# Scores turned out of PSUM by VectorE, and four kinds of work one to two places later, in a graph-attention kernel on one core

## The chip, the core and the metric

The kernel runs on one core of one Trainium2 chip. A core has five engines with in-order instruction streams: TensorE (PE in the profile, PEld for its weight loads), VectorE (DVE), ScalarE (ACT), GpSimd (POOL), and SyncE (SP), which here only starts transfers. On-chip memory is SBUF and, for the results of matmuls, PSUM in banks of 128 partitions by 512 fp32 values. The metric is the device time of one execution in microseconds; the time of a kernel is the median of several runs.

## The reference

A layer norm and a relu feed one graph-attention layer over 12,500 nodes with 128 features and 412,500 edges with 64 features, sorted by `dst`. One softmax runs over all edges.

```python
h = jnp.maximum(_layernorm(x, axis=-1), 0.0)
# inside, with node_features = h:
h = node_features @ Wn + bn
q = node_features @ Wq + bq
k = node_features @ Wk + bk
v = node_features @ Wv + bv
eh = edge_features @ We + be
attn_in = jnp.concatenate([q[src], k[tgt], eh], axis=-1)
hmid = jax.nn.leaky_relu(attn_in @ A1 + b1, 0.2)
scores = jax.nn.leaky_relu(hmid @ A2 + b2, 0.2)            # 8 heads
w = jax.nn.softmax(scores.mean(axis=-1), axis=0)           # over all edges
out = jax.ops.segment_sum(w[:, None] * v[tgt], src, num_segments=num_nodes)
y = h + out
return x + gamma * (y - mean(y)) / jnp.sqrt(var(y) + 1e-5) + beta
```

## The kernel before

**Nodes and edges.** Nodes are cut into 98 blocks of 128. Edges come in 403 groups of 1024 (`SUPER` = 8 tiles of 128 edges), and the groups are cut into 11 chunks (`CHUNKS`). Within a chunk each edge is sent to a slot of its source's block, so that the second half of the work can go block by block.

**Three jobs, interleaved.** While chunk c is in the first stage, the second stage handles chunk c-1 and the slot planning (`ready`) works out chunk c+1. Python writes the program in the order in which these jobs give up their turns: `interleave` takes one step at a time from the job that is least far along. Between 1010 and 5300 us all three run together.

- *First stage* (`first_stage`): a step makes half a group's row, two tiles of 128 edges. TensorE multiplies edge features (L993) and adds selected key and value rows (L996) in one PSUM bank; ScalarE evicts the bank to a ring of rows (`evict`: L977 writes the edges' places, L980 the bank), and POOL scatters the two tiles to the slot table in DRAM (L910). `Later` holds the eviction back for a number of first-stage steps. Three banks take turns: two of `row_ps` and `t_bank` (`next_bank`).
- *Slot planning* (`count`, `plan`, `place_slots`): one-hot products on TensorE (L476, L497, L553, L575), with VectorE building the operands (L469, L568) and reducing the result (L631).
- *Second stage* (`second_stage`): works through units of up to four blocks, nearly all of 12 slot tiles in three quads of four tiles. A unit's rows are loaded into `rows_of`, a ring of 72 tiles (SP, L1024).

**A unit's steps.** `second_stage` keeps a table: `at(when, turn, job)` puts a job at a place, and within a place the lower turn is written first, then the earlier unit. With `t` as twice the unit's start, a unit goes through: `places` and `put_places` (source places transposed on TensorE at L1040 through a bank of `next_bank`, copied out by ScalarE at L1045, sent round through DRAM); `select` (one-hot selection `sel_q`, VectorE, L1064); for each quad, two places apart, `turn` (TensorE transposes the rows, L1074, and adds the query rows, L1079, in one of two `h_ps` banks) and `steep` (leaky relu: ScalarE makes 0.2 times the value in the single buffer `low`, L1088; VectorE takes the larger of both, L1089, into `rows_of`). Then `heads_of` (TensorE, L1096: scores of 8 heads, and in a ninth column their weighted sum, into the single bank `s_ps`), `add_bias` (ScalarE, L1103: bank plus b2 to `z` in SBUF), `by_slot` (VectorE transposes 32x32 blocks, L1109, so that edges lie on partitions) and `scores` (VectorE, L1116 to L1124). `spread_top` and `greatest` (L1129, L1138) find the running maximum through `s_ps`, `exponentials` (ScalarE, L1151 and L1155) the weights of the edges. With `lag` places after the start, `weights` (VectorE, L1169: one-hot of the place times the weight, `w`), `products` (TensorE, L1182: values summed by node into `o_ps`) and `add_sums` (VectorE, L1198, or L1190 in the first chunk) follow quad by quad.

A place that ScalarE, VectorE or TensorE is given in this table is its place in that engine's own stream; the engines meet through semaphores alone. The table in the lines that the change touches (before):

```python
at(t + 2 * q, 1, turn, i, q)
at(t + 2 * q + 1, 0, steep, i, q)
t += 2 * nq                      # nq: quads of a unit
at(t - 1, 3, heads_of, i)
at(t, 0, add_bias, i)
at(t + 1, -1, by_slot, i)
at(t + 1, -1, scores, i)
at(t + 2, 2, spread_top, i)
at(t + 2, 3, greatest, i)
at(t + 3, 2, exponentials, i)
t = 2 * w["start"] + w["lag"]
at(t + 2 * q - 1, 0, weights, i, q)
at(t + 2 * q, 1, products, i, q)
```

## Time and profile before

| what | value |
|---|---|
| median of 3 runs | 5679.47 us (5656.46 to 5683.55) |
| the profiled execution | 5691.83 us, span 5690.1 us |
| mean granted TensorE clock | 0.878 |
| busy, share of the span | PE 78%, DVE 70%, POOL 57%, PEld 55%, ACT 37% |
| moved by DMA | 1316.86 MB, 231 GB/s |
| first chunk alone with the nodes | until about 930 us |
| both stages and slot planning | about 1010 to 5300 us |
| last chunk's second stage, output | from about 5430 us |

A group of instructions in the profile is shown as: line, engine, operation, tile written <- tiles read, shape and count; behind the bar its busy time and the mean length of one in ns; behind the second bar the time that the engine sat idle just before these instructions and what ended most of it ("<-DVE w L1169 171.3": 171.3 us ended when VectorE's w of line 1169 was there; "issue": nothing that the profile shows; "remote": an event of no known engine). An fp32 matmul is two matmul rows in the profile, and names are printed without their numbers (`a2_sb` as a_sb, `b2_col` as b_col).

### The profile page before, as it was taken

To read this page: it belongs to the slowest core of one execution; us is meant where nothing else is said; L and a number is where in the kernel's file an instruction comes from. 1 tells how busy PE (TensorE), PEld (TensorE's weight loads), DVE (VectorE), ACT (ScalarE), POOL (GpSimd) and SP (SyncE) were. 2 spreads that over 40 slices of the span, in tenths; PEclk is the share of its full clock that TensorE was granted. 3 is DMA by queue.
4 is the path that set the end of the run, shared out by engine and by line. 5 is a ranking of instruction groups with operands and counts; after the bars stand their busy time and mean duration, and the time that the engine had idled before them with its cause. 6 is when DMAs were issued, how large, how long until landed. Compare 5 with 4: busy or idle time off the path is not lost. (4 is left out here: it accounts for less than half of the span.)

```text
span 5690.1 us, 88351 instructions
## 1 busy us (share of the span) xinstructions
PE 4417.7 (78%) x27227; PEld 3125.2 (55%) x27227; DVE 3969.6 (70%) x12757; ACT 2087.2 (37%) x5599; POOL 3235.7 (57%) x3250
## 2 busy tenths in 40 slices
PE   6766656787788787788878778778778777778898
PEld 4433334555555555555555556556556555556674
DVE  6777534777677766666776776776777676667898
ACT  2333322333333333333333333333333333334456
POOL 3556566666566666665656655665665665665510
PEclk8888867998889888888888988988888988889999
DMA  4657667777777777776777777776776776778985
GB/s 127 187 189 212 207 191 243 237 248 227 229 240 246 224 251 232 238 234 220 244 229 240 242 230 235 239 241 219 244 243 225 250 235 211 245 242 278 300 280 205
DMA packets 659520, 1316.86 MB, mean 231 GB/s; under 512 B 112886, under 2 KB 310443, under 8 KB 659023
## 3 DMA queue, kind: packets, MB, share of 16 engines
q1 hardware_dynamic: 453248, 848.70, 49.2%
q0 software_dynamic: 154704, 424.26, 19.9%
q10 hardware_dynamic: 51071, 38.02, 2.1%
q8 instruction: 220, 3.60, 0.3%
q14 instruction: 277, 2.27, 0.1%
HBM read 820.50 MB, written 490.10 MB: 230 GB/s over the span
## 5 line engine op out<-in xcount | busy, mean ns | idle before, releaser
L910 POOL DMA_INDIRECT tab<-row,slots x3223 | 3232.6, 1003 | 2206.2 <-ACT row L980 940.6
L1182 PE MATMUL o_ps<-rows_of,w 128*128 128x128 f32 x6860 | 1024.6, 294 | 320.9 <-DVE w L1169 184.0
L1182 PEld LDWEIGHTS o_ps<-rows_of,w 128*128 128x128 f32 x6860 | 917.9, 203 | 446.4 <-issue 204.1
L1169 DVE TENSOR_SCALAR w<-iota_f,rows_of,score 128x128 f32<-128x128 f32 x3381 | 954.8, 356 | 0.2 <-issue 0.2
L1089 DVE TENSOR_TENSOR rows_of<-h_ps,low 128x512 f32<-128x512 f32 (+1 forms) x861 | 589.3, 684 | 510.0 <-ACT low L1088 324.1
L980 ACT ACTIVATE row<-row_ps 128x512 f32<-128x512 f32 x1151 | 681.1, 594 | 681.6 <-remote 212.1
L1088 ACT ACTIVATE low<-h_ps 128x512 f32<-128x512 f32 (+1 forms) x861 | 512.2, 595 | 1099.4 <-remote 352.1
L993 PE MATMUL row_ps<-w_ea,ea_t 128*128 128x256 f32 x2302 | 811.6, 437 | 102.8 <-ACT row L980 69.3
L1079 PE MATMUL h_ps<-sel_q,qw 128*128 128x128 bf16 (+3 forms) x4242 | 769.8, 315 | 11.5 <-issue 11.3
L993 PEld LDWEIGHTS row_ps<-w_ea,ea_t 128*128 128x128 f32 x2302 | 429.5, 214 | 344.4 <-issue 182.5
L1096 PE MATMUL s_ps<-rows_of,a_sb 128*32 128x384 f32 (+2 forms) x2392 | 316.6, 608 | 353.8 <-DVE rows_of L1089 231.7
L1074 PE MATMUL h_ps<-ident,rows_of 128*128 128x128 f32 x3430 | 583.7, 296 | 8.5 <-issue 7.9
L996 PEld LDWEIGHTS <-sel 126*128 126x128 bf16 x3224 | 343.6, 107 | 296.8 <-issue 78.1
L1074 PEld LDWEIGHTS h_ps<-ident,rows_of 128*128 128x128 f32 x3430 | 456.3, 154 | 86.4 <-issue 45.8
L1079 PEld LDWEIGHTS <-qw 128*128 128x128 bf16 x4242 | 413.6, 104 | 142.3 <-issue 51.0
L996 PE MATMUL row_ps<-kv,sel 126*128 126x256 bf16 x2302 | 486.7, 295 | 5.7 <-issue 4.7
L1103 ACT ACTIVATE z<-s_ps,b_col 128x384 f32<-128x384 f32 (+1 forms) x299 | 169.6, 567 | 787.6 <-PE s_ps L1096 426.3
L631 DVE TENSOR_REDUCE num<-run 128x5 f32<-128x490 f32 (+1 forms) x648 | 425.5, 657 | 10.3 <-PE run L575 4.5
L970 DVE TENSOR_SCALAR sel<-offs,third 126x512 bf16<-126x512 uint8 x806 | 361.1, 489 | 68.2 <-remote 35.7
L575 PE MATMUL run<-one,rest_b 128*128 128x500 f16 x637 | 262.6, 412 | 177.2 <-DVE num L631 108.1
L1138 DVE TENSOR_SCALAR_CACHE_REDUCE s_ps<-s_ps,less_of 128x128 f32<-128x128 f32 x298 | 106.1, 356 | 410.3 <-PE o_ps L1182 110.0
L1064 DVE TENSOR_SCALAR sel_q<-pls,part 128x512 bf16<-128x512 uint8 (+1 forms) x837 | 366.4, 490 | 0.7 <-issue 0.7
(247 smaller groups left out, 4816.4 us busy)
## 6 DMA issues: line engine op xcount, KB each, us to landing
rows_of<-tab SPq DMA_DIRECT2D x264, 1542.0 KB
ea_t<-in_ea SPq DMA_DIRECT2D x403, 256.0 KB
qw<-q_tab SPq DMA_DIRECT2D x192, 384.0 KB
tab<-row,slots POOLq DMA_INDIRECT x3223
offs<-off_d SPq DMA_DIRECT2D x403, 126.0 KB
pls<-pl_d SPq DMA_DIRECT2D x264, 192.0 KB
rows_of<-tab SPq DMA_DIRECT2D x27, 1028.0 KB
qw<-q_tab SPq DMA_DIRECT2D x96, 288.0 KB
```

What stands on the lines that cost most here:

```text
L631: nc.vector.tensor_reduce(num, strips[:, :NTN, :m].rearrange("p b m -> p m b"), AX.X, ALU.max)
L910: i = nc.gpsimd.indirect_dma_start(out=tab[:, :], out_offset=bass.IndirectOffsetOnAxis(ap=slots[c][t // (8 * STR)][:m, t % (8 * STR):t % ( ...
L980: nc.scalar.activation(row[:, :, 1:ROW], bank, AF.Copy)
L993: nc.tensor.matmul(bank[:, :, 0:D], lhsT=ea_g[:, ts(k, P)], rhs=w_ea, start=True, stop=False, skip_group_check=True)
L996: nc.tensor.matmul(bank[:, b, :], lhsT=sel[:, ts(b * halves + k, P)], rhs=kv, start=False, stop=True, skip_group_check=True)
L1064: nc.vector.tensor_scalar(sel[:, a:b], plss[i][:, a:b], part1, None, op0=ALU.is_equal)
L1074: nc.tensor.matmul(h_ps[:, ts(j, P)], lhsT=rows_of[i][:, a + j, 1:D + 1], rhs=ident, is_transpose=True, start=j == 0, stop=False, skip_gro ...
L1079: nc.tensor.matmul(h_ps[:, (x0 - a) * P:(x1 - a) * P], lhsT=qws[i][:, s, ts(k, D)], rhs=plss[i][:, x0 * P:x1 * P], start=False, stop=k == ...
L1088: nc.scalar.activation(low, h_ps, AF.Copy, scale=SLOPE)
L1089: nc.vector.tensor_max(rows_of[i][:, a:b, 1:D + 1], h_ps.rearrange("p (j e) -> p j e", j=m), low.rearrange("p (j e) -> p j e", j=m))
L1169: nc.vector.tensor_scalar(w, iota_f, rows_of[i][:, t, 0:1], state["score", i][:, t:t + 1], op0=ALU.is_equal, op1=ALU.mult)
L1182: nc.tensor.matmul(state["o_ps"][:, ts(t // ct, D)], lhsT=w, rhs=rows_of[i][:, t, D + 1:ROW], start=t == 0, stop=t % ct == ct - 1, skip_gr ...
```

## The change

VectorE's transpose reads the scores from `s_ps` itself; ScalarE's step with b2 and the tile `z` are gone. b2 (with the weighted sum as ninth value) lies in all partitions as `b2_all`, and VectorE adds it to nine of every 32 columns behind the transpose. In the table, `steep` moves from one to two places behind its `turn`; `heads_of` moves two places later, `by_slot` and `scores` one, `spread_top`, `greatest` and `exponentials` two; `lag`, and with it `weights`, `products` and `add_sums`, becomes 2nq+7 in all chunks, where it was 2nq+5 in all but the last. Rows of units with more than two quads are loaded two places later. In the first stage the eviction is written two steps behind its matmuls instead of one, except in the first chunk.

```diff
-        lag = 2 * nq + (7 if c == NC - 1 else 5)
+        lag = 2 * nq + 7
...
-    b2_col = const.tile([P, 1], FP, name="b2_col")
+    b2_all = const.tile([P, H + 1], FP, name="b2_all")
...
-        nc.tensor.matmul(t_bank[:, 0:1], lhsT=b2_row.rearrange("p g h -> p (g h)"), rhs=ones[0:1, 0:1], start=True, stop=True)
-        nc.vector.tensor_copy(b2_col, t_bank[:, 0:1])
+        nc.tensor.matmul(t_bank[:, 0:H + 1], lhsT=ones[0:1, :], rhs=b2_row[:, 0:H + 1], start=True, stop=True)
+        nc.vector.tensor_copy(b2_all, t_bank[:, 0:H + 1])
...
-                later.after(1, lambda g=g, k=k, bank=bank: evict(g, k, bank))
+                later.after(1 if chunk_of[g] == 0 else 2, lambda g=g, k=k, bank=bank: evict(g, k, bank))
...
-        def add_bias(i):
-            n = 32 * units[i]["n"]
-            state["z"] = p3.tile([P, most_tiles * 32], FP, name="z")
-            nc.scalar.activation(state["z"][:, 0:n], state["s_ps"][:, 0:n], AF.Identity, bias=b2_col)
-
         def by_slot(i):
-            nc.vector.transpose(state["zt"][:, 0:n], state["z"][:, 0:n])
+            nc.vector.transpose(state["zt"][:, 0:n], state["s_ps"][:, 0:n])
...
-            zt = state["zt"][:, 0:32 * n].rearrange("p (t h) -> p t h", h=32)
+            zt = state["zt"][:, 0:32 * n].rearrange("p (t h) -> p t h", h=32)[:, :, 0:H + 1]
+            nc.vector.tensor_add(zt, zt, b2_all.unsqueeze(1).to_broadcast([P, n, H + 1]))
...
-                at(t + 2 * q + 1, 0, steep, i, q)
-            t += 2 * nq
+                at(t + 2 * q + 2, 0, steep, i, q)
+            t += 2 * nq + 2
...
-        t = 2 * w["start"] - (19 if w["nq"] > 2 else 17)
+        t = 2 * w["start"] - 17
```

The order of instructions shows what this does. The places are the same unit of the program before and after, where a chunk with quads of four tiles passes into one with quads of three. On TensorE before, from the last turn of a unit (`h_ps_36061`) to its heads (`s_ps`):

```order
L1079 MATMUL h_ps_36061<-sel_q_35872,qw_7833 128x384
L993 MATMUL row_ps_36076<-w_ea_200,ea_t_35643 128x2x128
...
L1182 MATMUL o_ps_36083<-rows_of_7832,w_36059 128x128
L1096 MATMUL s_ps_7834<-rows_of_7832,a2_sb_193 32x384 x4
L1074 MATMUL h_ps_36116<-ident_74,rows_of_7832 128x128 x3
```

and after, from the last turn of that unit (`h_ps_35852`):

```order
L1078 MATMUL h_ps_35852<-sel_q_35666,qw_7827 128x384
...
L1177 MATMUL o_ps_35727<-rows_of_7826,w_35847 128x128
...
L1073 MATMUL h_ps_35927<-ident_74,rows_of_7826 128x128 x3
...
L1177 MATMUL o_ps_35942<-rows_of_7826,w_35920 128x128
L1095 MATMUL s_ps_7828<-rows_of_7826,a2_sb_193 32x384 x4
L1039 MATMUL row_ps_35952<-ident_74,rows_of_7826 12x128
```

A whole turn of the next unit and another group of products now stand between a unit's last turn and its heads, and the heads stand in one place with `places` (L1039). On VectorE before, from the last w ahead of that unit's last max (L1089, out of `h_ps_36061`) on:

```order
L1169 TENSOR_SCALAR w_36059<-iota_f_154,rows_of_7832,score_35948 128x128
L1089 TENSOR_TENSOR rows_of_7832<-h_ps_36061,low_36080 128x4x128
L1064 TENSOR_SCALAR sel_q_36093<-pls_35911,part1_168 128x512
...
L1169 TENSOR_SCALAR w_36110<-iota_f_154,rows_of_7832,score_35948 128x128
L556 TENSOR_TENSOR run_36144<-run_36144,carry0_144 128x490
...
L1109 STREAM_TRANSPOSE zt_36161<-z_36112 128x384
L1116 TENSOR_TENSOR none_36163<-slot_of4_114,filled0_140 128x12
```

and after:

```order
L1164 TENSOR_SCALAR w_35920<-iota_f_154,rows_of_7826,score_35781 128x128
L1088 TENSOR_TENSOR rows_of_7826<-h_ps_35852,low_35922 128x4x128
L504 TENSOR_TENSOR filled3_143<-run_35902,carry0_144 128x98
...
L1164 TENSOR_SCALAR w_35968<-iota_f_154,rows_of_7826,score_35781 128x128
L1103 STREAM_TRANSPOSE zt_35970<-s_ps_7828 128x384
L1110 TENSOR_TENSOR none_35972<-slot_of4_114,filled0_140 128x12
L1114 TENSOR_TENSOR zt_35970<-zt_35970,b2_all_196 128x12x9
```

The max still follows a w and the transpose still follows the next ones; what moved is TensorE's side, and the transpose now reads TensorE's bank. On ScalarE before, around the copy of the places (L1045):

```order
L1103 ACTIVATE z_36112<-s_ps_7834,b2_col_196 128x384
L980 ACTIVATE row_255<-row_ps_36076 128x2x256
L1088 ACTIVATE low_36171<-h_ps_36116 128x384
L977 ACTIVATE row_255<-place1_233 128x4
L980 ACTIVATE row_255<-row_ps_36127 128x2x256
L1045 ACTIVATE plT0_36202<-t_bank_213 12x128
L1048 DMA pl_d_67<-plT0_36202 12x128
L980 ACTIVATE row_255<-row_ps_36183 128x2x256
```

and after (TensorE's order there is `t_bank`, the turn `h_ps_35927`, `row_ps_35938`, `places` in `row_ps_35952`, the turn `h_ps_35987`):

```order
L1087 ACTIVATE low_35981<-h_ps_35927 128x384
L1044 ACTIVATE plT0_35984<-row_ps_35952 12x128
L1047 DMA pl_d_67<-plT0_35984 12x128
L976 ACTIVATE row_252<-place1_230 128x4
L979 ACTIVATE row_252<-t_bank_213 128x2x256
L979 ACTIVATE row_252<-row_ps_35938 128x2x256
L1087 ACTIVATE low_36057<-h_ps_35987 128x384
```

z is gone, and the evictions of `t_bank` and `row_ps_35938` stand behind the copy of the places, whose matmul TensorE issues after theirs.

14 lines of the change are left out of this document (6 added, 8 removed).

## The prediction

> **What bounds the kernel now.** I read the page's shares, then the busy time by stretch, then for the longest stretch the instructions grouped by line for TensorE (PE), VectorE (DVE) and ScalarE (ACT), and last the order in time of one stall. By stretch (length, then busy microseconds of PE, weight loads, DVE, ACT, POOL; granted clock, DMA share, GB/s):
>
> ```profile
> 1010.00:5300.00 4290.00, 3415.36 (x21841) 2479.59 (x21842) 3017.07 (x9638) 1529.16 (x3928) 2596.01 (x2584) 0.89 0.73 238
> 5300.00:5430.00 130.00, 116.59 (x911) 92.48 (x910) 107.57 (x340) 55.99 (x150) 71.69 (x72) 0.97 0.89 295
> 5430.00:5620.00 190.00, 168.23 (x1442) 135.44 (x1441) 172.30 (x597) 112.15 (x318) 6.37 (x7) 0.98 0.77 250
> ```
>
> Three quarters of the time is the first row, in which both stages and the slot planning run together. There PE is busiest (3415 of 4290 us) and yet idle for 875 us (20.4%); DVE is at 70%, ACT at 36%, POOL at 61%, the DMA engines at 73%. No engine is full: they wait for each other. The second row, where the slot planning is over, shows PE idle for only 10.3%, at a clock of 0.97 instead of 0.89, so neither DMA (0.89 there) nor DVE (83% there) holds PE at its present pace.
>
> PE's groups in the long stretch (after the bar: busy time, mean ns; idle time just before them and what ended it):
>
> ```profile
> L1182 PE MATMUL o_ps<-rows_of,w 128*128 128x128 f32 x5925 | 891.6, 295 | 300.0 <-DVE w L1169 171.3 <-issue 74.9 <-DVE acc L1198 25.6
> L993 PE MATMUL row_ps<-w_ea,ea_t 128*128 128x256 f32 x1726 | 592.7, 427 | 37.8 <-ACT row L980 30.6 <-issue 5.3 <-ACT plT L1045 1.5
> L1074 PE MATMUL h_ps<-ident,rows_of 128*128 128x128 f32 x2964 | 509.0, 298 | 7.8 <-issue 7.2 <-PE t_bank L996 0.3
> L993 PE MATMUL t_bank<-w_ea,ea_t 128*128 128x256 f32 x856 | 296.5, 431 | 18.1 <-ACT row L980 11.5 <-issue 6.0 <-ACT plT L1045 0.6
> L1096 PE MATMUL s_ps<-rows_of,a_sb 128*32 128x384 f32 (+2 forms) x2008 | 279.6, 636 | 328.2 <-DVE rows_of L1089 207.6 <-issue 113.5 <-DVE num L631 4.6
> L575 PE MATMUL run<-one,rest_b 128*128 128x500 f16 x463 | 186.5, 403 | 120.2 <-DVE num L631 72.8 <-issue 39.7 <-DVE s_ps L1138 5.4
> ```
>
> The largest wait is at the heads (L1096), 328 us in 251 units (2008 matmuls, 8 to a unit): 1.31 us each, for the leaky values that DVE writes at L1089. Next the products (L1182), 300 us for w. What DVE and ACT wait for:
>
> ```profile
> L1089 DVE TENSOR_TENSOR rows_of<-h_ps,low 128x512 f32<-128x512 f32 (+1 forms) x744 | 509.0, 684 | 466.2 <-ACT low L1088 289.2 <-issue 170.1 <-ACT row L980 2.5
> L1198 DVE SCALAR_TENSOR_TENSOR acc<-acc,fade_of,o_ps 128x512 f32<-128x512 f32 (+3 forms) x246 | 156.7, 645 | 161.9 <-remote 58.4 <-PE row_ps L996 36.9 <-PE run L575 22.4
> L1109 DVE STREAM_TRANSPOSE zt<-z 128x384 f32<-128x384 f32 (+2 forms) x251 | 141.3, 563 | 103.0 <-ACT z L1103 87.2 <-issue 15.6
> L1138 DVE TENSOR_SCALAR_CACHE_REDUCE s_ps<-s_ps,less_of 128x128 f32<-128x128 f32 x252 | 89.9, 357 | 396.4 <-PE o_ps L1182 108.0 <-remote 64.4 <-PE h_ps L1079 59.5
> L1103 ACT ACTIVATE z<-s_ps,b_col 128x384 f32<-128x384 f32 (+2 forms) x251 | 144.6, 576 | 731.5 <-PE s_ps L1096 379.0 <-PE o_ps L1182 78.6 <-PE h_ps L1079 49.8
> ```
>
> So it is a ring: PE turns a quad, DVE waits for ACT's part of it (466 us at L1089), PE then waits for DVE at the heads, ACT waits for the heads at z with evictions queued behind it. One such stall in order of time (start, duration, engine and line, idle before):
>
> ```profile
> 3153.88 1.30 PE L1182 MATMUL o_ps<-rows_of,w 128*128 128x128 f32 x8 [1.31 <-DVE w L1169]
> ...
> 3155.39 0.95 DVE L970 TENSOR_SCALAR sel<-offs,third 126x512 bf16<-126x512 uint8 x2
> ...
> 3156.26 0.68 DVE L1089 TENSOR_TENSOR rows_of<-h_ps,low 128x512 f32<-128x512 f32 x1
> ...
> 3156.99 1.51 PE L1096 MATMUL s_ps<-rows_of,a_sb 128*32 128x384 f32 x8 [1.81 <-DVE rows_of L1089]
> ```
>
> Here DVE is the late one: it turns out sel before the leaky values, and PE has nothing it may do.
>
> **The change, part by part.** All times are in the long stretch unless said; the sum is made against the profiled execution, 5691.83 us (span 5690.1), 12 us above the median of 5679.47.
>
> *Leaky values and heads later.* A quad's max comes two places behind its turn instead of one, and the heads one place behind the last max instead of in its own place. That takes away the direct hop of L1096. What remains is what a one-place gap leaves now: w at L1169 stands one place ahead of the products, and these wait 300.0 us in 741 groups (5925/8), 0.40 each. For 251 heads that is 100 us. Bounds: 328 saved if nothing waits; nothing saved if PE is held by DVE's total work. I take the one-place price, as heads now follow the products directly and DVE's max follows that quad's w: **-228**.
>
> *DVE's own waits.* With two places between turn and max, most of the 466 us at L1089 should go: DVE gains up to 1.9 us a unit, PE 0.9. DVE so gets ahead of PE relative to today, which shortens the wait for w. Against it stands that PE now reaches the products sooner. Bounds: 300 saved, or 228 added (the heads' whole gain coming back). I take a fifth of the 300: **-60**.
>
> *z leaves ACT.* 144.6 us of ACT work and 731.5 us of its waiting vanish; ACT at 36% bounds nothing, so this is worth nothing by itself. But DVE now waits for the heads with its own queue (scores, max, w behind it), one place behind them. The nearest row is L1198, which waits for PE's products one place back: 161.9 us, against 103.0 that L1109 waits now. The 59 us more fall on DVE's idle time, which this stretch has in plenty (1273 us): nothing on the path, its cover being that PE has a turn and a row group to do meanwhile; 59 without it.
>
> *Transposing out of PSUM and the added b2.* Rows of the same size by form:
>
> ```profile
> L1109 DVE STREAM_TRANSPOSE zt<-z 128x384 f32<-128x384 f32 x264 | 150.3, 569 | 104.2 <-ACT z L1103 87.6 <-issue 15.6 <-ACT row L980 0.8
> L1190 DVE COPY acc<-o_ps 128x384 f32<-128x384 f32 x32 | 17.6, 551 | 22.9 <-remote 14.5 <-PE row_ps L996 3.9 <-PE row_ps L993 2.4
> L505 DVE TENSOR_TENSOR filled<-run,carry 128x98 f32<-128x98 f32 x10 | 2.6, 255 | 7.2 <-issue 4.2 <-PE run L497 1.9 <-PE row_ps L996 1.1
> ```
>
> A copy of 384 columns out of PSUM takes 551 ns where the transpose out of SBUF takes 569, so the source costs nothing that these rows show. [...] The add of 12x9=108 columns goes by L505 (98 columns, 255 ns): 0.27 us by 299, about 80 us of DVE. It is on the path only while DVE paces PE; PE's idle share, 20%, says how often: **+16** (bounds 0 and 80).
>
> *Evictions one place later.* A row bank comes round after three takes, and `places` takes one per unit. Without it an eviction stands one place ahead of the matmul that needs its bank (two before); for the two row groups behind each `places` it now stands in the same place. L993 waits 37.8+18.1=56 us in 1291 groups today. Lower bound: nothing more; upper: each of the 502 groups waits like today's heads, 1.31 us, 658. ACT is half as busy as DVE and loses the stall at z, so I stay near the low end, the present wait once more: **+56**. POOL's scatters shift along; POOL is idle for 39% of the stretch.
>
> *Loads two places later.* rows_of (L1024) moves two places on SP, past the first stage's loads there. It is issued long before its first use:
>
> ```profile
> 3017.17 0.39 SPq L1024 DMA_DIRECT2D rows_of<-tab  x1
> ...
> 3042.52 0.27 PE L1040 MATMUL t_bank<-ident,rows_of 128*12 128x128 f32 x1
> ```
>
> Eight places are 25.4 us, so six are about 19; 1542 KB at the stretch's 238 GB/s is an estimated 6.5 us. Nothing, its cover being those 19 us; if gone, PE would wait at L1040 with all behind it. The start comes two places sooner to its first turn and the last chunk starts two later: nothing net. Three of four b2 loads less at the start: nothing, the weights' loads are waited for there.
>
> *Last chunk.* Its lag was 7 already, so there the scores have less room ahead of w, and DVE is the busier engine (172.3 of 190 us). 25 units by the add's 0.27 is 7, plus a little for the room: **+10**.
>
> *The clock.* Idle PE costs twice. In the stretch with 10.3% idle the same matmuls are shorter:
>
> ```profile
> L1182 PE MATMUL o_ps<-rows_of,w 128*128 128x128 f32 x287 | 41.0, 285 | 2.7 <-DVE w L1169 1.3 <-DVE acc L1198 0.9 <-PE h_ps L1079 0.5
> L1074 PE MATMUL h_ps<-ident,rows_of 128*128 128x128 f32 x144 | 22.6, 280 | 0.0
> L993 PE MATMUL row_ps<-w_ea,ea_t 128*128 128x256 f32 x48 | 15.1, 397 | 0.0
> L1096 PE MATMUL s_ps<-rows_of,a_sb 128*32 128x384 f32 x96 | 10.4, 506 | 10.7 <-DVE rows_of L1089 9.7 <-issue 1.0
> ```
>
> 295 to 285, 298 to 280, 427 to 397, 636 to 506: about 6% for 0.08 of clock. The terms so far take 216 us of idle time away, leaving 659 of 4074 (16.2%), four tenths of the way to 10.3%: 2.5% of 3415 us, **-85** (bounds 0 and -205). [...]
>
> Sum: -228-60+16+56+10-85 = -291, so 5401 for a profiled execution and **5390** as a median.
>
> **The rivals.** *Row banks (slower).* PE stands at L993 (now L992) behind `places` for an eviction queued behind low and plT on ACT. For it: 30.6 and 11.5 us of L993's wait end with ACT row even with two places of room. Against: ACT idles 64%. Without the term of 56 the gain is 347, over 502 groups 0.69 us: from there on it decides. At 1.0 us each: 5692-347+502-12 = 5835.
> *The wait only moves.* DVE's total work paces PE, so the heads' wait returns at the products and `run`, and only costs stay: 5692+16+10-12 = 5706. For it: in the stall shown DVE never idles. Against: DVE idles 1273 us of the stretch, 466 at L1089.
> *The ring opens.* PE idles as from 5300 to 5430, at that clock: 3415 less 6% is 3210, over 0.897 is 3579, 711 less: 4969. For it: the same instructions do it there. Against: the slot planning's L631 and L575 hop (120 us) is not touched.
>
> **Chances.** The forecast 0.63, with its own range 5150 to 5600 from the bounds above; banks 0.17; moved wait 0.10; open ring 0.10. Range 5150 to 5720: it leaves out most of the open ring and of the banks, under 0.2 together. Changes within 0.5% (28 us) I count as none, about what three runs here can tell. Faster 0.73 (forecast and open ring), same 0.06 (over half of the moved wait), slower 0.21.
>
> **What would show it.** Right: the heads' wait near 100 us, L1089's far under 466, the L992 rows near 110, the add near 270 ns, the transpose still near 569, granted clock over 0.90. Wrong: L992 waits of several hundred us ended by ACT row; or the products' wait risen by what the heads lost; or L1040 waiting for its load.

## The result, and the profile after

The changed kernel takes 5771.69 us (median of 4 runs, 5763.93 to 5778.22) where the kernel before took 5668.35 us beside it: a ratio of 1.0173, 95% interval 1.0149 to 1.0197. It is slower; the forecast was 5390 us and faster. The profiled execution took 5778.22 us, its span 5776.5 us, its mean granted clock is 0.884 (before 0.878).

The same work fills the long stretch until 5385 us instead of 5300 us; 85 of the 86 us by which the span grew are there. Its busy times (columns as in the prediction), and PE's groups in it, in the kernel after (the lines of the changed code have numbers lower by one to five):

```profile
1010.00:5385.00 4375.00, 3446.79 (x21872) 2471.78 (x21871) 3055.47 (x9870) 1363.01 (x3672) 2566.43 (x2582) 0.89 0.72 234
```

```profile
L1177 PE MATMUL o_ps<-rows_of,w 128*128 128x128 f32 x5939 | 941.9, 306 | 351.3 <-DVE w L1164 158.5 <-issue 126.1 <-DVE acc L1193 35.4
L1078 PE MATMUL h_ps<-sel_q,qw 128*128 128x384 bf16 (+3 forms) x3622 | 661.9, 311 | 150.0 <-DVE sel_q L1063 87.1 <-issue 55.4 <-DVE left L614 3.6
L992 PE MATMUL row_ps<-w_ea,ea_t 128*128 128x256 f32 x1720 | 577.3, 418 | 106.7 <-ACT row L979 50.9 <-issue 29.8 <-ACT plT L1044 24.9
L1073 PE MATMUL h_ps<-ident,rows_of 128*128 128x128 f32 x2968 | 492.6, 288 | 58.8 <-issue 35.5 <-DVE rows_of L1088 17.2 <-DVE w L1164 3.9
L992 PE MATMUL t_bank<-w_ea,ea_t 128*128 128x256 f32 x862 | 294.1, 424 | 52.4 <-ACT row L979 35.6 <-issue 16.2
L1095 PE MATMUL s_ps<-rows_of,a_sb 128*32 128x384 f32 (+1 forms) x2008 | 261.4, 588 | 9.8 <-issue 3.6
L574 PE MATMUL run<-one,rest_b 128*128 128x500 f16 x461 | 189.6, 411 | 121.8 <-DVE num L630 80.6 <-issue 27.1 <-DVE s_ps L1133 7.0
```

The query rows' matmuls, the second part of a turn, in the kernel before (1010 to 5300 us):

```profile
L1079 PE MATMUL h_ps<-sel_q,qw 128*128 128x384 bf16 (+3 forms) x3606 | 671.3, 319 | 10.2 <-issue 10.0
```

PE is idle for 4375 - 3447 = 928 us, where it was 875. The heads (L1095) no longer wait: 9.8 us instead of 328. As much waiting, and a little more, stands elsewhere. The turns (L1078, L1073) wait 209 us, where L1074 had 7.8 and L1079 10.2; the products 351 instead of 300; the row groups (L992, two rows) 159 instead of 56. Of the turns' 209 us, 87 end with `sel_q` on DVE, which nobody had moved, and 91 with nothing that the profile shows. DVE and ACT in the kernel after:

```profile
L1088 DVE TENSOR_TENSOR rows_of<-h_ps,low 128x512 f32<-128x512 f32 (+1 forms) x744 | 506.7, 681 | 181.4 <-ACT low L1087 120.1 <-issue 61.3
L1193 DVE SCALAR_TENSOR_TENSOR acc<-acc,fade_of,o_ps 128x512 f32<-128x512 f32 (+3 forms) x247 | 157.5, 645 | 221.2 <-remote 178.6 <-PE h_ps L1078 12.3 <-PE t_bank L995 8.9
L1103 DVE STREAM_TRANSPOSE zt<-s_ps 128x384 f32<-128x384 f32 (+1 forms) x251 | 143.7, 573 | 247.7 <-remote 98.0 <-PE s_ps L1095 35.6 <-PE h_ps L1078 30.0
L1133 DVE TENSOR_SCALAR_CACHE_REDUCE s_ps<-s_ps,less_of 128x128 f32<-128x128 f32 x251 | 89.3, 356 | 372.5 <-PE o_ps L1177 121.9 <-PE s_ps L1124 87.6 <-remote 67.6
L1114 DVE TENSOR_TENSOR zt<-zt,b_all 128x108 f32<-128x108 f32 (+1 forms) x251 | 68.1, 271 | 0.0
L1146 ACT ACTIVATE score<-score,less_of 128x12 f32<-128x12 f32 (+2 forms) x251 | 76.2, 304 | 793.5 <-DVE s_ps L1133 414.6 <-issue 282.5 <-DVE rows_of L1088 44.6
```

The same on DVE: the leaky values (L1088) wait 285 us less than before, the scores' transpose (L1103) 145 us more and the sums (L1193) 59 us more. The full-size transpose by itself, over the whole run:

```profile
L1103 DVE STREAM_TRANSPOSE zt<-s_ps 128x384 f32<-128x384 f32 x264 | 152.8, 579 | 242.4 <-remote 104.7 <-PE s_ps L1095 31.7 <-PE h_ps L1078 27.0
```

ACT's 731 us at z are gone; at the weights of the edges it now waits 793 us (L1146), where it waited 88 (L1151 before).

Most of the rows' wait is at one place. Counted from each `places` (L1039) on, the second row group waits 124 of the 159 us and all others 35. 87 of the 159 us end with ACT's eviction, in 57 waits of 1.5 us on average. One of them, on PE and on ACT:

```profile
3675.88 0.28 PE L1039 MATMUL row_ps<-ident,rows_of 128*12 128x128 f32 x1
3680.12 0.70 PE L992 MATMUL t_bank<-w_ea,ea_t 128*128 128x256 f32 x2 [1.79 <-ACT row L979]
```

```profile
3678.83 0.27 ACT L1044 ACTIVATE plT<-row_ps 12x128 uint8<-12x128 f32 x1 [3.46 <-PE h_ps L1078]
3679.47 0.60 ACT L979 ACTIVATE row<-t_bank 128x512 f32<-128x512 f32 x1 [0.37 <-ACT plT L1044]
```

The matmul L992 needs `t_bank`, which ACT evicts (L979) behind the copy of the places (L1044); ahead of the copy ACT is idle for 3.46 us. Over the 57 waits ACT is idle ahead of L1044 for 31 us and evicts for 34 us, and none of that time lies ahead of L1146. What the copy waits for is not settled: its own matmul (L1039) was through 2.7 us earlier here.

### The profile page after: what moved, and what is told of

Its sections match the earlier page's. It is cut to its first block, busy times and chain, and to the rows that moved or that the text cites. A ratio compares the mean times of both kernels' runs of the same rounds, so it can differ in the third digit from the quotient of the medians.

```text
span 5776.5 us, 88648 instructions
## 1 busy us (share of the span) xinstructions
PE 4451.4 (77%) x27227; PEld 3111.7 (54%) x27227; DVE 4023.7 (70%) x13056; ACT 1895.1 (33%) x5300; POOL 3207.9 (56%) x3250
## 5 line engine op out<-in xcount | busy, mean ns | idle before, releaser
L1177 PE MATMUL o_ps<-rows_of,w 128*128 128x128 f32 x6860 | 1073.5, 303 | 376.7 <-DVE w L1164 178.6
L1177 PEld LDWEIGHTS o_ps<-rows_of,w 128*128 128x128 f32 x6860 | 968.5, 213 | 496.3 <-issue 257.4
L992 PE MATMUL row_ps<-w_ea,ea_t 128*128 128x256 f32 x2304 | 804.1, 433 | 178.6 <-ACT row L979 84.0
L1078 PE MATMUL h_ps<-sel_q,qw 128*128 128x128 bf16 (+3 forms) x4242 | 758.8, 308 | 152.6 <-DVE sel_q L1063 87.6
L979 ACT ACTIVATE row<-row_ps 128x512 f32<-128x512 f32 x1152 | 674.7, 591 | 547.2 <-remote 248.2
L1088 DVE TENSOR_TENSOR rows_of<-h_ps,low 128x512 f32<-128x512 f32 (+1 forms) x861 | 586.5, 681 | 212.9 <-ACT low L1087 147.5
L1073 PE MATMUL h_ps<-ident,rows_of 128*128 128x128 f32 x3430 | 567.0, 287 | 76.3 <-issue 36.2
L992 PEld LDWEIGHTS row_ps<-w_ea,ea_t 128*128 128x128 f32 x2304 | 423.4, 214 | 306.8 <-ACT row L979 105.8
L1078 PEld LDWEIGHTS <-qw 128*128 128x128 bf16 x4242 | 402.1, 101 | 306.3 <-issue 213.1
L1073 PEld LDWEIGHTS h_ps<-ident,rows_of 128*128 128x128 f32 x3430 | 437.0, 149 | 150.9 <-issue 70.5
L574 PE MATMUL run<-one,rest_b 128*128 128x500 f16 x637 | 267.1, 419 | 174.9 <-DVE num L630 102.9
L567 DVE TENSOR_TENSOR one<-bins_b,near 128x500 f16<-128x500 bf16 (+1 forms) x648 | 301.1, 465 | 128.4 <-remote 31.0
L1146 ACT ACTIVATE score<-score,less_of 128x12 f32<-128x12 f32 (+1 forms) x299 | 90.7, 303 | 859.0 <-DVE s_ps L1133 471.3
```

What stands on the lines that cost most here:

```text
L979: nc.scalar.activation(row[:, :, 1:ROW], bank, AF.Copy)
L992: nc.tensor.matmul(bank[:, :, 0:D], lhsT=ea_g[:, ts(k, P)], rhs=w_ea, start=True, stop=False, skip_group_check=True)
L1073: nc.tensor.matmul(h_ps[:, ts(j, P)], lhsT=rows_of[i][:, a + j, 1:D + 1], rhs=ident, is_transpose=True, start=j == 0, stop=False, skip_gro ...
L1078: nc.tensor.matmul(h_ps[:, (x0 - a) * P:(x1 - a) * P], lhsT=qws[i][:, s, ts(k, D)], rhs=plss[i][:, x0 * P:x1 * P], start=False, stop=k == ...
L1088: nc.vector.tensor_max(rows_of[i][:, a:b, 1:D + 1], h_ps.rearrange("p (j e) -> p j e", j=m), low.rearrange("p (j e) -> p j e", j=m))
L1177: nc.tensor.matmul(state["o_ps"][:, ts(t // ct, D)], lhsT=w, rhs=rows_of[i][:, t, D + 1:ROW], start=t == 0, stop=t % ct == ct - 1, skip_gr ...
```

## The experiments

18 runs of 12 kernels in five batches; each batch ran on one chip with its own runs of the kernel before, and every ratio is to those. That matters: the kernel before took 5774.63, 5686.21, 4745.49, 4725.52 and 5688.65 us in the five. In the first, second and fifth batch it ran as in the result (called the *long* batches below), in the third and fourth it took a sixth less (the *short* ones). Long or short does not belong to the chip: the first and the third batch ran on the same one, and the others on three more. What this says of the hardware is told last; until then ratios are compared among long batches, or among short ones.

The theory at the start: late evictions make the two row groups behind each `places` wait for their bank (the prediction's first rival), and cost more than the other parts give. The rivals: that VectorE paces TensorE and the heads' wait has only moved, or that VectorE's scores are to blame (it has more to do). The expectations of the first batch are in microseconds, for a kernel before at 5668; it took 5774.63 there, so a time of 5670 us is 0.982 of the kernel before in that batch, and not 1.000.

### The parts one by one (first batch)

The changed kernel with its evictions put back:

```diff
-                later.after(1 if chunk_of[g] == 0 else 2, lambda g=g, k=k, bank=bank: evict(g, k, bank))
+                later.after(1, lambda g=g, k=k, bank=bank: evict(g, k, bank))
```

> The changed kernel with evictions one step behind their matmuls again; all else as changed. Theory 'late evictions' (TensorE stands at the row matmuls for a bank whose eviction is now queued later; that wait rose from 56 to 159 us): the row matmuls' wait falls back to about 60 us and the time to about 5670, as before the change. Theory 'the waits moved' (VectorE paces TensorE; the heads' 328 us came back at the products, at the turns and at the rows alike): the row wait falls, other waits take it over, 5740 to 5775. Theory 'VectorE's extra work' (80 us of adds, and its own wait at the transpose): unchanged, 5760 to 5780.

Measured: 5670.6 us, 0.9831 of before (0.9803 to 0.9859): the first theory's time, and by the ratio below all three. The kernel before with the late evictions alone (the same line, the other way round):

> The kernel before with evictions two steps behind (first chunk as before). Late evictions: slower by most of the 103 us, 5740 to 5780, with the row matmuls' wait near 160. The waits moved, or VectorE's work: 5650 to 5690, as before.

Measured: 5912.09 us, 1.0232 (1.0195 to 1.027). Its row groups in its long stretch (1010 to 5515 us):

```profile
L993 PE MATMUL row_ps<-w_ea,ea_t 128*128 128x256 f32 x1738 | 617.7, 440 | 155.5 <-ACT row L980 122.2 <-ACT plT L1045 17.3 <-issue 14.8
L993 PE MATMUL t_bank<-w_ea,ea_t 128*128 128x256 f32 x860 | 306.9, 442 | 93.0 <-ACT row L980 84.5 <-issue 7.5 <-ACT low L1088 0.8
```

248 us where the kernel before waits 56, and 207 of them end with ACT's eviction (L980): more wait and more time than any of the three gave. So this part alone makes the kernel slower, by 137 us in one and the same batch. The kernel before with the places alone:

```diff
-        lag = 2 * nq + (7 if c == NC - 1 else 5)
+        lag = 2 * nq + 7
...
-                at(t + 2 * q + 1, 0, steep, i, q)
-            t += 2 * nq
+                at(t + 2 * q + 2, 0, steep, i, q)
+            t += 2 * nq + 2
...
-        t = 2 * w["start"] - (19 if w["nq"] > 2 else 17)
+        t = 2 * w["start"] - 17
```

> The kernel before with the leaky values two places behind their turns and everything behind them two places later, z still on ScalarE, evictions as before. My prediction's ring: 5400 to 5500, since the heads' wait goes and nothing takes its place. The waits moved: heads' wait near 10 us, turns' and products' waits up by about as much, 5640 to 5720. Late evictions or VectorE's work: 5660 to 5690 or lower, since neither is in it.

Measured: 5714.75 us, 0.9914 (0.9881 to 0.9946). The heads' wait falls to 9 us and the turns' (L1079, L1074) rises to 251, as the moved waits have it. But DVE's wait at the leaky values, which two places between turn and max were to take away, rises from 466 us (1010 to 5300 us):

```profile
L1089 DVE TENSOR_TENSOR rows_of<-h_ps,low 128x512 f32<-128x512 f32 (+1 forms) x743 | 506.9, 682 | 637.2 <-ACT low L1088 460.1 <-issue 139.4 <-ACT z L1103 21.0
```

The kernel before with the scores out of PSUM and the added b2 alone; as z's place is free, the scores stand one place earlier than before:

```diff
-            nc.vector.transpose(state["zt"][:, 0:n], state["z"][:, 0:n])
+            nc.vector.transpose(state["zt"][:, 0:n], state["s_ps"][:, 0:n])
...
+            nc.vector.tensor_add(zt, zt, b2_all.unsqueeze(1).to_broadcast([P, n, H + 1]))
...
-            at(t, 0, add_bias, i)
-            at(t + 1, -1, by_slot, i)
-            at(t + 1, -1, scores, i)
+            at(t, 0, by_slot, i)
+            at(t, 0, scores, i)
```

> The kernel before with the transpose out of PSUM and the add of b2 on VectorE, in the place after the heads; leaky values, heads and evictions as before. VectorE's extra work: slower by 40 to 100 us, 5710 to 5770, the transpose's wait up from 103 to about 250 us. Late evictions: as before, 5650 to 5690. The waits moved: VectorE has 80 us more to do and paces TensorE, plus 20 to 80, 5690 to 5750.

Measured: 5740.29 us, 0.9931 (0.991 to 0.9952). Both other parts make the kernel a little faster, each by under 1%, and together (the first run) by 1.7%. So VectorE's extra work is not what makes the change slower. The moved waits are there, but what they take away is the gain that was foreseen. By the prediction's sum without its term for evictions these parts were to bring 347 us. They bring 104 in this batch, and where the rest went stands in the groups of PE in the changed kernel with evictions put back (1010 to 5300 us):

```profile
L1177 PE MATMUL o_ps<-rows_of,w 128*128 128x128 f32 x6008 | 931.8, 301 | 306.6 <-DVE w L1164 186.1 <-issue 69.4 <-DVE acc L1193 14.9
L1078 PE MATMUL h_ps<-sel_q,qw 128*128 128x128 bf16 (+3 forms) x3547 | 650.6, 311 | 177.2 <-DVE sel_q L1063 80.0 <-issue 75.0 <-DVE sel L969 4.8
L992 PE MATMUL row_ps<-w_ea,ea_t 128*128 128x256 f32 x1732 | 575.2, 414 | 52.5 <-ACT plT L1044 25.3 <-issue 22.1 <-ACT row L979 4.2
L1073 PE MATMUL h_ps<-ident,rows_of 128*128 128x128 f32 x3004 | 491.8, 286 | 78.4 <-issue 41.4 <-DVE rows_of L1088 32.1 <-DVE top_of L1119 2.7
L992 PE MATMUL t_bank<-w_ea,ea_t 128*128 128x256 f32 x870 | 283.4, 409 | 11.0 <-issue 5.8 <-ACT plT L1044 3.7 <-ACT row L979 1.3
```

The row groups are back at 64 us; but the turns wait 256 us, most of what the heads had waited.

### The parts in pairs (second batch)

The changed kernel unchanged, on another chip:

> The changed kernel itself, on the chip of these runs, so that all combinations of the three parts have the same neighbour. Late evictions: about 3% above the one with evictions one step behind (0.983 of before), so 1.01 to 1.02 of before. Nothing else is asked of it.

Measured: 5788.95 us, 1.0195 (1.0151 to 1.0239). The changed kernel with the places put back (late evictions and scores on VectorE stay):

> The changed kernel with leaky values, heads and all behind them back in their old places; evictions late, scores on VectorE. Late evictions as a cost that adds to the others: 1.023 (late evictions alone) times 0.993 (scores alone) of before, 1.015 to 1.02. Late evictions as a cost by what stands ahead of them on ScalarE (low waits there for a turn just issued, and the eviction behind it): as large as alone or larger, 1.015 to 1.03. Waits moved: no more than the changed kernel, 1.01 to 1.02.

Measured: 5813.78 us, 1.0224 (1.0176 to 1.0271). The changed kernel with z on ScalarE again (late evictions and places stay):

> The changed kernel with z and b2 back on ScalarE, a place behind the heads; evictions late, leaky values late. Costs that add: 1.023 times 0.991 of before, 1.01 to 1.018. If low ahead of the evictions is what makes late evictions dear, late leaky values take that away (low no longer waits for the turn just issued): 0.99 to 1.005.

Measured: 5848.82 us, 1.0302 (1.026 to 1.0345). Both values expected of this one, 1.01 to 1.018 and 0.99 to 1.005, are missed by more than 1%: the parts do not simply add, and a `low` that need not wait for the turn just issued does not make late evictions cheap. Beside the changed kernel of the same batch, moving z off ScalarE brings 60 us and the places 25. In this kernel, too, DVE waits 538 us at L1089, 413 of them until `low` is there; the changed kernel beside it waits 153. So in each of the four settings of the other two parts the late evictions cost: 1 to 1.0232, 0.9914 to 1.0302, 0.9931 to 1.0224, and 0.9831 to 1.0173 or 1.0195. That is 2.3% to 3.9%, some 130 to 220 us; pairs from two batches are compared by their ratios to their own kernel before, so these differences carry the spread of two batches. In microseconds they are 73 to 137. The sign is the same in all, the size is known only so far.

The fourth kernel asks whether the turns' wait is a cost of its own. It is the kernel with evictions put back, and `sel_q` written one place earlier on VectorE:

```diff
-            at(t - 1, 3, select, i)
+            at(t - 2, 3, select, i)
```

> The changed kernel with evictions one step behind (0.983 of before), and the one-hot selection sel_q one place earlier, so two places ahead of the turns that need it. In that kernel the turns wait 160 us at L1078 and 75 us at L1073, mostly for sel_q. If these are where the heads' wait went and sel_q's place is what holds PE: the turns' wait falls under 60 us and the time to 0.96 to 0.97 of before. If VectorE's total work holds PE: the wait goes on to the products or the slot planning, 0.978 to 0.988.

Measured: 5633.16 us, 0.9908 (0.9878 to 0.9937). Its groups, 1010 to 5300 us:

```profile
L1177 PE MATMUL o_ps<-rows_of,w 128*128 128x128 f32 x6058 | 936.4, 298 | 325.3 <-DVE w L1164 175.9 <-issue 73.0 <-DVE acc L1193 30.2
L1078 PE MATMUL h_ps<-sel_q,qw 128*128 128x384 bf16 (+3 forms) x3702 | 672.0, 313 | 71.1 <-issue 37.1 <-DVE sel_q L1063 27.9 <-DMA offs<-off_d 3.7
L574 PE MATMUL run<-one,rest_b 128*128 128x500 f16 x463 | 186.3, 402 | 199.7 <-DVE num L630 121.5 <-issue 57.9 <-DVE one L567 7.5
```

The wait at L1078 fell from 177 to 71 us (that at L1073 rose from 78 to 94), and the time did not fall to the 0.96 to 0.97 that was to follow: the slot planning's matmuls (L574, the row shown) wait 200 us instead of 147, the products 325 instead of 307. So PE waits for DVE at other lines that ask for it. Whether the edit gains or loses a little is open: the kernel without it ran in the other batch, with a lower ratio (0.9831) and a longer time (5670.6). Beside the changed kernel of its own batch, with late evictions, it is 156 us faster.

### The price of single terms (third batch, a short one)

The kernel with evictions put back, once more:

> The changed kernel with evictions one step behind, once more beside the two that follow, on their chip. Costs that add: 0.98 to 0.985 of before, as in its first run.

Measured: 4798.43 us, 1.0105 (1.009 to 1.0121): slower here, where it was faster in the first batch, on the same chip. The same with half of b2 added twice, which leaves the result as it is and costs one more add for each unit:

```diff
-        nc.vector.tensor_scalar(b2_row, b2_row, bend / H, None, op0=ALU.mult)
+        nc.vector.tensor_scalar(b2_row, b2_row, bend / H / 2, None, op0=ALU.mult)
...
-            nc.vector.tensor_add(zt, zt, b2_all.unsqueeze(1).to_broadcast([P, n, H + 1]))
+            for _ in range(2):
+                nc.vector.tensor_add(zt, zt, b2_all.unsqueeze(1).to_broadcast([P, n, H + 1]))
```

> The changed kernel with evictions one step behind, and half of b2 added twice: 299 more adds of 0.27 us on VectorE, 80 us in all, in the chain from heads to weights. My term for one such add was 16 us of the path, between 0 and 80. VectorE paces TensorE: 50 to 90 us above the run without it. The engines share the path as their idle time says: 10 to 30 us.

Measured: 4817.68 us, 1.0155 (1.0142 to 1.0169): 19 us more than its neighbour for about 80 us more of VectorE (299 adds of 0.271 us). The prediction's price for one add was 16.

The changed kernel with a small addition: evictions still stand two steps late, but when `places` takes a bank, all that are held back come one step forward. The row groups behind `places` are so spared the eviction in their own place. Two evictions are held back at each `places`, so about 500 of the stretch's 1291 are brought forward, and the others stay late.

```diff
+    def hurry(self):
+        soon = self.todo
+        self.todo = {}
+        for when, jobs in sorted(soon.items()):
+            for job in jobs:
+                if when == self.now + 1:
+                    job()
+                else:
+                    self.todo.setdefault(when - 1, []).append(job)
...
             state["turned", i] = bank = next_bank(units[i]["c"] + 1)
+            held_back[0].hurry()
```

> The changed kernel, evictions two steps behind, but when places takes a bank out of turn the evictions still held back are written one step sooner: so no row matmul needs a bank whose eviction stands in its own step. In the changed kernel the second row group behind places waits 114 us, 240 times, and all others together some 30. Late evictions through the banks' rotation: that wait falls under 40 us and the time to 0.98 to 0.995 of before. Late evictions through something else (ScalarE's order, scatters bunched on POOL): wait down, time still 1.01 to 1.02.

Measured: 4745.41 us, 1.0001 (0.9992 to 1.001). The wait that was to fall under 40 us did not: the second row group behind `places` waits 63 us, the rows 102 in all (1010 to 4400 us; 50 and 106 in the changed kernel of the next batch). And the kernel before with `t_bank` kept for `places`, so that rows take turns in two banks and a row group always needs its bank one place behind its eviction:

```diff
-        taken[0] += 1
-        if c > 0 and taken[0] % 3 == 0:
-            return t_bank
...
-            state["turned", i] = bank = next_bank(units[i]["c"] + 1)
+            state["turned", i] = bank = t_bank
```

> The kernel before with t_bank for places alone and rows turning between the two row_ps banks: evictions stay one step behind, but each is needed in the next step instead of one or two later. Late evictions through the banks: row waits of several hundred us, since all of 1291 groups now have one step, 1.01 to 1.06 of before. If only a bank needed in the eviction's own step hurts: row waits under 100 us and 0.99 to 1.01.

Measured: 4742.43 us, 0.9995 (0.9985 to 1.0004), with 45 us of row waits. One place between an eviction and the matmul that needs its bank costs nothing here. In this batch no version is more than 1.6% from the kernel before, in either direction, and these runs can't tell bank reuse from lateness.

### Bank reuse, or lateness as such (fourth and fifth batch)

Fourth batch, again a short one: the changed kernel, the one with evictions put back, the one that hurries them, and the kernel before with late evictions alone.

> The changed kernel, as the measure for the three beside it. If this batch runs as the result did (before near 5680 us, POOL's scatters not back to back): 1.017 to 1.020 of the kernel before. If it runs as the third batch did (before near 4745 us, scatters back to back at 1.27 us for nearly the whole stretch, 3223 of them or 4083 us): 0.995 to 1.015, since then POOL's queue paces all versions.

Measured: 4722.1 us, 0.9992 (0.998 to 1.0003).

> The changed kernel with evictions at one place as before. Row-banks theory: where scatters are not back to back, 0.980 to 0.986 of the kernel before, the row matmuls L992 waiting under 70 us; where they are, 1.00 to 1.01. Rival (the gain of the first batch was that chip's alone): 1.00 to 1.02 on any chip.

Measured: 4769.63 us, 1.0087 (1.007 to 1.0104).

> The changed kernel, with every eviction in hand brought one place forward when places takes a bank, all others two places late. Row-banks theory (only the row groups behind places pay): most of the gain of a_evict1_third over after_third, so 0.980 to 0.995 of before where scatters are not back to back; rows' waits in the stretch under half of the 159 us of the changed kernel. Rival (an eviction late is dear as such, by ACT's queue, the scatters or the row ring behind it): within 0.5% of after_third. Where scatters are back to back: 1.00, as in the third batch.

Measured: 4716.27 us, 0.9974 (0.9964 to 0.9983).

> The kernel before with late evictions alone. Row-banks theory: 1.02 to 1.027 of before where scatters are not back to back, rows' waits near 250 us. Where they are back to back: within 1% of before, the rows' waits lying beside POOL's queue.

Measured: 4743.52 us, 1.0032 (1.002 to 1.0045). The late evictions alone cost 0.3% here and 2.3% in the first batch; the whole change costs nothing here.

In both short batches the kernel with evictions put back is slower than before by about 1%, and its trace says where. One place in it, on ACT, POOL and PE (start, duration, engine and line, idle before):

```profile
2832.54 0.21 ACT L976 ACTIVATE row<-place 128x4 f32<-128x4 uint8 x1 [11.99 <-DMA tab<-row,slots]
2832.65 0.25 ACT L1044 ACTIVATE plT<-t_bank 12x128 uint8<-12x128 f32 x1
```

```profile
2829.80 0.96 POOL L909 DMA_INDIRECT tab<-row,slots  x1 [0.30 <-issue]
2834.65 0.96 POOL L909 DMA_INDIRECT tab<-row,slots  x1 [3.89 <-ACT row L979]
```

```profile
2832.95 1.22 PE L992 MATMUL t_bank<-w_ea,ea_t 128*128 128x256 f32 x2 [8.24 <-ACT plT L1044]
```

ACT stands 12 us before it writes into the ring of rows, until the scatters already issued have landed; the copy of the places stands behind it, PE behind that, and POOL runs dry. There are nine such stalls of 10 to 16 us, one in nearly every chunk, each a group and a half ahead of the next chunk's first scatter; the three others of the batch have none of over 9 us there. Nine times 12 is more than the 44 us by which this kernel is behind the one before. Why ACT there waits for the newest scatters, and not for those that last used its place in the ring, is open.

Fifth batch, a long one again. The kernel that hurries:

> The changed kernel with evictions hurried where places takes a bank, on a third chip. If the kernel before takes 5650 to 5780 us there (scatters not back to back): by the row-banks theory 0.980 to 0.995 of it, the rows' waits in the long stretch under 100 us; by the rival (late evictions dear as such) 1.012 to 1.024, as the changed kernel had. If it takes 4720 to 4750 us: 0.996 to 1.001 again, which tells nothing new.

Measured: 5684.44 us, 0.9986 (0.9963 to 1.0009). The kernel before, for its trace beside it:

> The kernel before, unchanged, for a trace of it beside the other. Ratio 1.00. If it takes 4720 to 4750 us: scatters back to back for 85 to 95% of the stretch, waits of PE for the heads near 170 us where the first trace has 328, and nearly none that end with no releaser. If it takes 5650 to 5780 us: the waits of the first trace again within 15%.

Measured: 5684.37 us, 0.9986 (0.9962 to 1.0009). The changed kernel's groups in the second batch, and the hurrying one's here (1010 to 5300 us both, though the former's long stretch lasts until about 5385; in the latter L1005 are the row groups, L1191 the products):

```profile
L1177 PE MATMUL o_ps<-rows_of,w 128*128 128x128 f32 x5760 | 916.9, 307 | 346.1 <-DVE w L1164 137.2 <-issue 127.3 <-DVE acc L1193 50.3
L992 PE MATMUL row_ps<-w_ea,ea_t 128*128 128x256 f32 x1688 | 566.5, 419 | 96.3 <-ACT row L979 48.3 <-issue 25.2 <-ACT plT L1044 22.4
L992 PE MATMUL t_bank<-w_ea,ea_t 128*128 128x256 f32 x850 | 289.3, 424 | 56.2 <-ACT row L979 38.3 <-issue 17.4
```

```profile
L1191 PE MATMUL o_ps<-rows_of,w 128*128 128x128 f32 x5945 | 945.1, 302 | 231.6 <-issue 118.0 <-DVE w L1178 82.8 <-DVE acc L1207 11.0
L1005 PE MATMUL row_ps<-w_ea,ea_t 128*128 128x256 f32 x1721 | 580.3, 420 | 47.1 <-issue 35.0 <-ACT plT L1058 9.5 <-ACT row L992 1.8
L1005 PE MATMUL t_bank<-w_ea,ea_t 128*128 128x256 f32 x864 | 294.3, 423 | 20.0 <-issue 11.6 <-ACT plT L1058 5.0 <-ACT row L992 2.9
```

What the eviction ends of the row groups' waits falls from 87 to 5 us, the whole wait from 152 to 67 (the kernel before waits 56 and, in its second trace, 73), and the kernel goes from 1.017 or 1.020 to 0.999 of the kernel before. So in the long batches the rows' added wait is the bank reuse behind `places`, and bringing forward the evictions in hand there takes the loss against the kernel before away; the two kernels ran in different batches. If every late eviction cost the same wherever it stands, bringing forward 500 of 1291 would take back 39% of the way from 1.017 or 1.020 to 0.983 and leave an estimated 1.004 or 1.005; the measured 0.9986 with its interval (to 1.0009) is below that. The expectation of 0.980 to 0.995 is missed by a little, and the rival's 1.012 to 1.024 by more. Left over is the distance to 0.983, the kernel with all evictions early in the first batch. In microseconds little is left: 5772 and 5789 for the change, 5684 with the evictions hurried, 5671 with all early. Whether the rest is lateness as such or the first batch, in which the kernel before was 1.5% slower than in the two other long ones, isn't settled. In the short batches the same edit left the rows' wait where it was (102 and 100 us, 106 in the changed kernel), and why is open. Nor does the rows' wait give the size: late evictions add 192 us of it to the kernel before and 95 to the kernel with places and scores changed, and cost 137 us there and 101 or 118 here. No version that ran in both kinds of batch beats the kernel before in both: the hurrying one is at 0.9974 to 1.0001 of it.

## Why the prediction was wrong, point by point

The forecast of 5390 was 382 us too low. Two steps failed, the first by more: the price of the wait that stays once the heads are moved, and the term for the late evictions. The split below takes the 0.983 of the first batch, and is as good as that.

- *Leaky values and heads later, -228.* The heads' wait did go, to 9.8 us and not to 100. What failed is the step "For 251 heads that is 100 us", which priced the wait that stays at the place from which it was taken. The wait went to the next places at which PE asks DVE for something, the turns (209 us after, 256 with the evictions put back) and the products. With the terms for DVE's own waits and for the clock, the forecast without its evictions was 347 us faster than before; the kernel that has just these parts was faster by 104 us. That is some 240 us of the miss. Also, only 208 of the heads' 328 us ended with the leaky values; 114 ended with nothing that the profile shows, and such waits stand at the turns now (91 us). It is the rival *The wait only moves*, for its greater part, and it had a chance of 0.10.
- *DVE's own waits, -60.* L1088 fell from 466 to 181 us, but not for the reason given. With two places between turn and max alone it rises to 637, and with late evictions as well to 538; with z off ScalarE alone it stays (468). It falls where both are done (181, 184 with the evictions put back): in the new places `low` comes late as long as ScalarE makes z too. The number was met by luck, and L1103 and L1193 took up 204 of the 285 us. DVE idles 4375 - 3055 = 1320 us against 1273.
- *z leaves ACT, 0, and the transpose and the add, +16.* The durations were right: the add takes 271 ns (foreseen 0.27 us), the transpose out of PSUM 579 where it was 569 out of SBUF, for the same size: 10 ns more, by which all 299 transposes take an estimated 3 us more. The add's price was right too (19 us measured for a second one, in a short batch). But this part alone came out at 0.9931, a gain of 34 us by medians, not a loss of 16, and in the new places it brought 44 and, with late evictions, 60 us within a batch. So "worth nothing by itself" for z was wrong by some 50 us or more. In the new places the trace shows a way, `low` waiting behind z; in the old ones the shorter way from heads to scores is the likely place, and no run tells it apart from the rest of this part.
- *Evictions one place later, +56.* Mechanism and place were named (the rival *Row banks*), the size was off. The waits at L992 rose by 103 us, 44 of them ended by ACT's eviction, and the time by 2.3% to 3.9%, 130 to 220 us. In microseconds it is 73 to 137; either way it is more than 56. The step that failed is "so I stay near the low end": ACT at a third of its time was taken for an ACT that is there when it is needed. An eviction goes in ACT's order, and the late ones stand behind the copy of the places, ahead of which ACT is idle for 31 of the 87 us that PE waits for evictions. Nor did ACT lose its stall at z, as the term has it: 731 us there became 793 at L1146, though this stall is not the one that holds these evictions. Why the time rises by as much as it does, with 103 us more of row waits, stays open.
- *Loads two places later, 0.* Nearly right: in the long batches 7 to 25 us of L1039's waits end with its load in the kernels with the new places, and less than 1 in the kernel before.
- *The clock, -85.* It was to follow from less idle time. PE's idle share went from 20.4% to 928 / 4375 = 21.2%, and the granted clock stayed: 0.89 in the stretch, before and after. That "idle PE costs twice" was read from stretches alone: 0.89 at 20.4% idle and 0.97 at 10.3% in the kernel before, and 0.96 at 10.3% in the short batch's stretch shown last (3042 of 3390 us busy). No run changed the idle time alone, so that the idle time sets the clock is not shown.

The section on what would show it named the right line for this ("the products' wait risen by what the heads lost"), but only for one place; it was the turns.

## What to carry to other kernels

Where no engine is full and the engines wait for each other, a wait that is taken away at one place can come back at the next places that ask the same engine, as it did here: 318 us of PE's idle time left the heads, and the sum of it went from 875 to 928 us. Price an edit by that sum, and not by the wait that it removes. When work on a ring of banks is moved later, look for the user that comes round most quickly, here the row groups behind an extra taker, and for what then stands ahead of the release in its engine's order, here the copy of the places. And run a change in more than one batch before its sign is believed: the same kernel was 1.7% faster and 1.1% slower than the kernel before on one and the same chip.

## What the runs showed of the hardware

The same program took 5668 to 5775 us in some batches and 4726 to 4745 us in others, and on one chip 5775 us in one batch and 4745 us in another less than an hour later. The long stretch of the kernel before in the fifth batch (5676.6 us), and of the kernel before with late evictions in the fourth (4744.6 us), first by stretch, then POOL's scatters:

```profile
1010.00:5300.00 4290.00, 3401.46 (x21882) 2469.50 (x21882) 3013.28 (x9634) 1523.24 (x3930) 2590.05 (x2583) 0.89 0.75 238
```

```profile
1010.00:4400.00 3390.00, 3042.24 (x21485) 2286.27 (x21478) 2940.28 (x9426) 1474.09 (x3853) 2561.16 (x2527) 0.96 0.89 295
```

```profile
L910 POOL DMA_INDIRECT tab<-row,slots x2583 | 2590.3, 1003 | 1701.0 <-ACT row L980 788.0 <-issue 682.7 <-ACT plT L1045 116.3
```

```profile
L910 POOL DMA_INDIRECT tab<-row,slots x2527 | 2561.2, 1014 | 829.1 <-issue 565.5 <-ACT row L980 83.5 <-DMA tab<-row,slots 81.0
```

The engines' work is the same (DVE 313 and 312 ns for an instruction on average, POOL 1003 and 1014 ns for a scatter, PE 294 and 283 ns for a matmul of the products, at a granted clock of 0.89 and 0.96). What differs is the idle time. In the short batch POOL issues scatter upon scatter, 2561 us busy and 566 us of its own between them: 92% of the stretch, where it is 76% in the long one. That would leave little for anything else to lengthen, and fits that one and the same change costs 1.7% to 2.0% in the long batches and nothing in the short ones. That POOL's queue is the bound there is read from this share alone, and no run took scatters away. And the products of both:

```profile
L1182 PE MATMUL o_ps<-rows_of,w 128*128 128x128 f32 x5939 | 893.8, 294 | 321.0 <-DVE w L1169 179.4 <-issue 71.3 <-DVE acc L1198 34.3
```

```profile
L1182 PE MATMUL o_ps<-rows_of,w 128*128 128x128 f32 x5824 | 810.7, 283 | 68.8 <-DVE w L1169 68.1
```

In the long batches PE, DVE and ACT have waits that nothing in the profile ends ("issue", "remote"), 71 us in this one group; in the short batch's row all but 0.7 of its 68.8 us end with w. All three engines are idle at once for 295 us of the first kernel's stretch and for 34 us of the second's; in the changed kernel's stretch (long) it is 421 us. What holds them in the long batches was not found: no run here takes away a suspect, and the transferred bytes and packets are the same but for 2 of 659,520 packets.
